# Half products in the output projection of a ViT block: seven instead of eight, with their first operands made in the last chunk of attention

## The chip, the cores and the metric

The kernel runs on one core of a Trainium2 chip. The number that counts is the device time of one execution in microseconds, as the median of three runs. The profile is of one further execution on the same kernel. Engines are called PE (matrix products), DVE (vector), ACT (activations), POOL (GpSimd) and SP (which issues transfers). All tensors are float32.

## The reference

Two layers follow each other on 48 x 48 = 2304 tokens with 768 channels. The first is a transformer block with 12 heads of 64 channels, softmax with relative positions, an output projection and an MLP. The second is a spectral layer (a two-dimensional Fourier transform, a small two-layer network on the modes, and the way back). What the change touches is the step from attention to the MLP:

```python
attn = softmax(q*scale @ k.T + rel_h + rel_w)
out = (attn @ v).transpose(...).reshape(B, H, W, C)
out = out @ proj_w + proj_b          # 2304 x 768 times 768 x 768
x = shortcut + out
xn2 = layernorm(x, ln2_g, ln2_b)
h = gelu(xn2 @ mlp_w1 + mlp_b1)
return x + (h @ mlp_w2 + mlp_b2)
```

## The kernel before, in words

The tokens lie in 18 tiles of 128 (`NT`), the channels in 6 (`NC`), and `CH` = 384 is half of the channels. `main` is one large buffer in SBUF. Through attention it holds exponentials (18 slots of 768 values per partition, `exps`), and then the tokens `x1`, tile n in the place of slot n. `shared` holds `xt` (transposed tokens) and `xs` (three sums of them). `oT` is a buffer in device memory with the output of attention, transposed.

**Attention** runs over 6 pairs of heads (`pr`), in each over 6 chunks of 384 queries (`c`), in each over two runs (`u`) of 9 key tiles: 72 runs. A run makes scores on PE (L525, L531), exponentials on ACT (L535) and one sum on DVE for every key tile but the first (`acc`, L592: 128x768, both inputs in SBUF). The products with the values (L540) of one run are issued in the next. `finish` closes a chunk one run later: `den` on PE (L555), a copy of it with its sum on ACT (L560), then on DVE `ot` (L564), a reciprocal (L567) and the scaled output `o` (L569), then on POOL the running sum `inverse` (L570), and on SP the store into `oT` (L571). The last chunk's `finish` stands after all products. The order of PE and SP inside attention is written by hand (a manual schedule); that of DVE, ACT and POOL is made by a scheduler. Each engine works through its own order without skipping.

**Projection.** For each token tile SP loads a tile of `oT` (`outputs`, `og`, L639, 384 KB) and a tile of x (`residual`, L632), and POOL adds the projection's bias to x (L633). `projected` makes two halves of 384 columns from six products each (L646; two instructions of PE stand behind each product in float32), and DVE adds each half from PSUM to `x1` (L650). Nine tiles (`EARLY`) are projected before a branch. The branch tests that all sums of exponentials and their inverses are below a bound (L666 to L679, on DVE with one transpose on PE), and if they are not, a generic path computes attention again; with this data it is skipped. After the branch the other nine tiles are projected, while tiles 0 to 5 are normalised (L116 to L124), transposed on PE (L132) and written into `xt`; `sums_of_tokens` makes their sums in `xs`. PE's order is written by hand before the branch.

**MLP.** It already forms its products by the scheme of seven half products: `left` makes the sums of one factor's four blocks and `right` those of the other's.

```python
def left(eng, a11, a12, a21, a22, s):
    eng.tensor_tensor(s[0], a21, a22, ALU.add)
    eng.tensor_tensor(s[1], s[0], a11, ALU.subtract)
    eng.tensor_tensor(s[2], a12, s[1], ALU.subtract)
    eng.tensor_tensor(a21, a11, a21, ALU.subtract)

def right(eng, b11, b12, b21, b22, t):
    eng.tensor_tensor(t[0], b12, b11, ALU.subtract)
    eng.tensor_tensor(t[1], b22, t[0], ALU.subtract)
    eng.tensor_tensor(t[2], b21, t[1], ALU.subtract)
    eng.tensor_tensor(b12, b22, b12, ALU.subtract)
```

Of the kernel before, what the change touches and what calls it, by code (L numbers as in the profile page):

```python
# [9 lines left out]
F32 = mybir.dt.float32  # L10
# [3 lines left out]
ALU = mybir.AluOpType  # L14
# [30 lines left out]
def block_then_afno(  # L45
# [139 lines left out]
    with ExitStack() as flag_scope:  # L185
# [9 lines left out]
        pw = col_parts.rearrange("p (c f) -> p c f", c=NC)  # L195

        with ExitStack() as att:
# [108 lines left out]
            def queries_keys_values(qkv):  # L306
# [17 lines left out]
                stage = qkv.enter_context(tc.tile_pool(name="qkv_out", bufs=7))  # L324
# [181 lines left out]
            with tc.manual_schedule(engines={mybir.EngineType.PE, mybir.EngineType.SP}):  # L506
# [44 lines left out]
                def finish(pr, c, acc, ot):  # L551
# [18 lines left out]
                    nc.gpsimd.tensor_tensor(inverse, inverse, rden, ALU.add)  # L570
# [6 lines left out]
                for n, (pr, c, u) in enumerate(runs):  # L577
# [4 lines left out]
                    if (c, u) == (4, 0) and pr == NC - 1:  # L582
                        nc.sync.dma_start(out=pw, in_=proj_w.rearrange("(c p) f -> p c f", p=P))
                    if u == 0:
                        acc = o_pool.tile([P, 2, G], F32, name="acc")
# [44 lines left out]
        def residual(t):  # L630

            nc.sync.dma_start(out=x1[:, t, :], in_=x[ts(t, P), :])  # L632
            nc.gpsimd.tensor_tensor(x1[:, t, :], x1[:, t, :], pb, ALU.add)  # L633

        def outputs(t, og=None):

            if og is None:
                og = pj.tile([P, NC, P], F32, name="og")
            nc.sync.dma_start(out=og, in_=oT[:, ts(t, P)].rearrange("(c p) t -> p c t", p=P))  # L639
            return og  # L640

        def projected(psum, t, og):
            for k in range(2):
                pp = psum.tile([P, CH], F32, name="pp", tag="o")
                for c in range(NC):
                    nc.tensor.matmul(  # L646
                        pp, og[:, c, :], pw[:, c, ts(k, CH)], start=(c == 0), stop=(c == NC - 1)
                    )
                half = x1[:, t, ts(k, CH)]
                nc.vector.tensor_tensor(half, pp, half, ALU.add)  # L650
# [3 lines left out]
        EARLY = NT // 2  # L654
        with tc.tile_pool(name="ps_flag", bufs=1, space=PSUM) as psum, tc.tile_pool(
            name="ps_early", bufs=2, space=PSUM
        ) as psum_early, tc.manual_schedule(engines={mybir.EngineType.PE}):
            early = {t: outputs(t) for t in range(3)}
            pb = pj.tile([P, C], F32, name="pb", bufs=1)
            nc.sync.dma_start(out=pb, in_=proj_b[0, :].partition_broadcast(P))  # L660
            b2 = pj.tile([P, C], F32, name="b2_early", bufs=1)
            nc.sync.dma_start(out=b2, in_=mlp_b2[0, :].partition_broadcast(P))
            residual(0)
            projected(psum_early, 0, early[0])
# [7 lines left out]
            for t in range(1, EARLY):  # L672
# [7 lines left out]
                residual(t)  # L680
                projected(psum_early, t, early[t] if t in early else outputs(t))
            for t in range(EARLY, NT):
                residual(t)
            later = {t: outputs(t) for t in range(EARLY, EARLY + 3)}
# [696 lines left out]
```

## Time and profile before

| | us |
|---|---|
| median of three runs | 3062.45 (3062.34 to 3068.3) |
| the profiled execution, its own time | 3062.51 |
| its span in the profile | 3060.7 |
| QKV, last matmul starts | 450.6 |
| attention, until the last `den` starts | 1522.8 |
| projection, first and last matmul start | 1524.3 and 1677.6 |
| MLP, first and last matmul start | 1678.9 and 2730.1 |
| spectral layer | to the end |

The profile gives for each engine its busy time, and for each group of equal instructions the line, the names of the tiles, the shape and the mean length. A row of a timeline has the start, the length of the group, engine, line, operation, tiles and count, and in brackets the idle time before it with the engine and line that ended the wait. A recorded length runs from the start of an instruction until it is done, and may hold time in which it could not go on. The granted PE clock in that execution was 0.987 of full speed on average.

### The profile page before, as it was taken

How to read it: one execution, taken by the hardware profiler on the slowest of the kernel's cores; microseconds unless marked ns; L12 is line 12 of the kernel's file. 1: busy time of each engine (PE TensorE's matmuls, PEld its weight loads, DVE VectorE, ACT ScalarE, POOL GpSimd, SP SyncE). 2: the span in 40 equal slices, each digit the busy share in tenths (PEclk: the TensorE clock that was granted, in tenths of full speed). 3: DMA queues.
4: the chain of work that ended last, by engine and by line, in shares of the span. 5: the costliest groups of instructions: out<-in, count | busy, mean ns of one | idle time of the engine just before them, and what ended most of it. 6: DMA issues, size and time to landing. Idle time of an engine off the chain costs nothing. (4 is left out here: it accounts for less than half of the span.)

```text
span 3060.7 us, 40413 instructions
## 1 busy us (share of the span) xinstructions
PE 2963.6 (97%) x15495; PEld 1796.0 (59%) x15495; DVE 1783.4 (58%) x2579; ACT 868.6 (28%) x1346; POOL 572.1 (19%) x510
## 2 busy tenths in 40 slices
PE   7999989999999999999999999989999999989998
PEld 4555645655556565555555555545555555548885
DVE  4243217777777777777624766666666566653443
ACT  1011115655556565555400211121101111011110
POOL 2203010000000000000133422342233222311210
PEclk9999999999999999999999999999999999999999
DMA  4433256173452617344332111121112211132324
GB/s 120 132 98 109 96 138 123 28 133 62 81 119 45 136 30 134 66 73 81 110 112 68 52 62 52 53 73 61 53 52 62 74 54 60 52 91 58 87 72 150
DMA packets 204144, 253.37 MB, mean 83 GB/s; under 512 B 21698, under 2 KB 185762, under 8 KB 202406
## 3 DMA queue, kind: packets, MB, share of 16 engines
q1 hardware_dynamic: 203942, 250.69, 32.5%
q8 instruction: 125, 2.05, 0.3%
q14 instruction: 77, 0.63, 0.1%
HBM read 136.77 MB, written 50.14 MB: 61 GB/s over the span
## 5 line engine op out<-in xcount | busy, mean ns | idle before, releaser
L592 DVE TENSOR_TENSOR acc<-acc,main 128x768 f32<-128x768 f32 x576 | 551.8, 958 | 202.6 <-ACT main L535 146.1
L535 ACT ACTIVATE main<-sp 128x768 f32<-128x768 f32 x648 | 522.1, 811 | 155.9 <-PE sp L531 148.6
L531 PE MATMUL sp<-terms,select 64*128 64x384 f32 x1296 | 411.9, 629 | 0.0
L989 DVE TENSOR_TENSOR main<-o,main 128x384 f32<-128x384 f32 x540 | 298.9, 556 | 43.2 <-PE o L987 4.8
L927 PE MATMUL h<-shared,w 128*128 128x384 f32 x864 | 297.1, 487 | 0.8 <-issue 0.8
L417 PE MATMUL m<-main 128*128 128x384 f32 x756 | 253.0, 495 | 23.9 <-DMA main<-in_qkv_w_dram 13.7
L525 PE MATMUL sp<-shared 64*128 64x384 f32 x1296 | 266.4, 488 | 1.6 <-ACT row_hi L223 1.0
L525 PE MATMUL sp<-qT,kT 64*128 64x384 f32 x1296 | 266.4, 487 | 0.0
L570 POOL TENSOR_TENSOR inverse<-inverse,rden 128x384 f32<-128x384 f32 x36 | 46.3, 1286 | 1032.6 <-DVE rden L567 968.9
L927 PEld LDWEIGHTS h<-shared,w 128*128 128x128 f32 x864 | 164.6, 191 | 116.3 <-issue 2.6
L927 PE MATMUL h<-shared,w1s 128*128 128x384 f32 x648 | 226.7, 486 | 0.0
L540 PE MATMUL op<-main,shared 128*64 128x384 f32 x1296 | 221.3, 488 | 0.0
L417 PEld LDWEIGHTS m<-main 128*128 128x128 f32 x756 | 144.4, 193 | 130.1 <-issue 26.1
L540 PE MATMUL op<-main,v 128*64 128x384 f32 x1296 | 220.0, 488 | 0.0
L933 ACT ACTIVATE hT<-c,vec 128x384 f32<-128x384 f32 x108 | 66.4, 615 | 466.5 <-DVE c L939 466.4
L939 DVE TENSOR_TENSOR c<-h,u 128x384 f32<-128x384 f32 x108 | 60.1, 557 | 212.4 <-PE h L927 212.4
L987 PE MATMUL o<-w,hT 128*128 128x384 f32 x432 | 176.3, 490 | 2.9 <-DVE mv L118 1.5
L987 PE MATMUL o<-w2s,hs 128*128 128x384 f32 x432 | 177.2, 492 | 1.0 <-DVE hs L153 1.0
L531 PEld LDWEIGHTS sp<-terms,select 64*128 64x128 f32 x1296 | 125.1, 186 | 83.9
L927 PEld LDWEIGHTS h<-shared,w1s 128*128 128x128 f32 x648 | 123.1, 190 | 85.9
L540 PEld LDWEIGHTS op<-main,v 128*64 128x64 f32 x1296 | 90.6, 138 | 106.4 <-issue 106.4
L525 PEld LDWEIGHTS sp<-shared 64*128 64x128 f32 x1296 | 116.9, 186 | 59.7 <-issue 20.3
(157 smaller groups left out, 3888.7 us busy)
## 6 DMA issues: line engine op xcount, KB each, us to landing
w<-in_mlp_w_dram SPq DMA_DIRECT2D x72, 768.0 KB
terms<-col_parts SPq DMA_DIRECT2D x432, 72.0 KB
terms<-row_hi SPq DMA_DIRECT2D x216, 72.0 KB
terms<-row_lo SPq DMA_DIRECT2D x216, 72.0 KB
main<-in_qkv_w_dram SPq DMA_DIRECT2D x36, 384.0 KB
z<-zt SPq DMA_DIRECT2D x48, 150.0 KB
z<-y SPq DMA_DIRECT2D x50, 144.0 KB
zo<-z SPq DMA_DIRECT2D x12, 600.0 KB
```

The source lines that it names most:

```text
L417: nc.tensor.matmul(bank, a[:, c, :], b[:, c, :], start=(first and c == 0), stop=(c == 2), skip_group_check=not first,)
L525: nc.tensor.matmul(sp[:, j, :G], kT[at, ts(kt, P)], qT[at, ts(c, G)], start=True, stop=False,)
L531: nc.tensor.matmul(sp[:, j, :G], select[at, a % 2], ready[pr, c][at, a // 2, b], start=False, stop=True,)
L535: nc.scalar.activation(p, sp[:, :, :G], AF.Exp, scale=HD**-0.5)
L540: nc.tensor.matmul(op[ts(j, 64)], v[:, kt0 + i, ts(j, 64)], ps[i][:, j, :], start=(kt0 + i == 0), stop=(kt0 + i == NT - 1),)
L570: nc.gpsimd.tensor_tensor(inverse, inverse, rden, ALU.add)
L592: nc.vector.tensor_tensor(acc, made[0] if kt == 1 else acc, p, ALU.add)
L927: nc.tensor.matmul(bank[i], a[:, c, :], b[:, c, :], start=(start and c == 0), stop=(c == 2), skip_group_check=not start,)
L933: nc.scalar.activation(h[:, i, ts(k, G)], src, AF.Gelu, bias=col(V_B1 + 2 * n + i))
L939: nc.vector.tensor_tensor(t, src, other, ALU.add)
L987: nc.tensor.matmul(bank[k], a, b, start=start, stop=True, skip_group_check=not start)
L989: nc.vector.tensor_tensor(dst, bank[k], dst, ALU.add)
```

## The change

The projection works on pairs of token tiles. For a pair, the outputs of attention are a 2 x 2 block matrix (token tile by half of the channels), and so are the weights `pw`; seven products of blocks take the place of eight, each of three matmuls, so 21 matmuls per pair instead of 24. PE makes them in four banks, `o0` to `o3`, of which the fifth, sixth and seventh product use `o0`, `o2` and `o3` a second time. The first product is copied to `u` by ACT, the second is added to `u` by DVE, the third and fourth are added into `x22`, then the second uses of the banks into `x11`, `x21` and `x12`, and at last `u` is added to three of the four quarters.

The sums that the products need are new work. The four sums of the weights (`right`) are made once, on POOL, in the last chunk of attention; they lie in `xs`, and `pw` and the bias `pb` are loaded three runs earlier. The outputs of tiles 0 to 3 are loaded in the last run into `xt`, and the four sums (`left`) of tiles 0 and 1 are made on POOL there. The `left` sums of the other eight pairs are made on DVE. The last chunk's `inverse` is added on DVE.

Ten tiles instead of nine are projected ahead of the branch. `sums_of_tokens` moves to the end of the projection, as `xs` is in use until then. In the first step of the MLP one product with its activation is issued earlier. Pools are reordered or made smaller (five store buffers instead of seven in QKV, fewer in the generic path), and the loads of `b2` and `rows_dft` are issued earlier with that.

The diff, without the parts in the generic path that only make buffers smaller:

```diff
--- before.py
+++ after.py
@@ -193 +193 @@
         pw = col_parts.rearrange("p (c f) -> p c f", c=NC)
+        b11, t3, b21, b22 = (pw[:, ds(3 * i, 3), ts(k, CH)] for i in range(2) for k in range(2))
+        t1, t2, t4 = (xs[:, k] for k in range(3))
+        pb = flag_pool.tile([P, C], F32, name="pb")
+
+        def residual(t):
+
+            nc.sync.dma_start(out=x1[:, t, :], in_=x[ts(t, P), :])
+            nc.gpsimd.tensor_tensor(x1[:, t, :], x1[:, t, :], pb, ALU.add)
+
+        def outputs(t, og):
+
+            nc.sync.dma_start(out=og, in_=oT[:, ts(t, P)].rearrange("(c p) t -> p c t", p=P))
+            return og
+
+        def sums_of_outputs(eng, og, ogs):
+
+            a = [og[i][:, ds(3 * k, 3)] for i in range(2) for k in range(2)]
+            s = [ogs[:, k] for k in range(3)]
+            left(eng, *a, s)
+            return *a, *s
+
+
+        first = [xt.rearrange("p c t -> p (c t)")[:, ts(i, C)] for i in range(4)]
+        first = [a.rearrange("p (c t) -> p c t", c=NC) for a in first]
+        first_parts = []
@@ -324 +349 @@
-                stage = qkv.enter_context(tc.tile_pool(name="qkv_out", bufs=7))
+                stage = qkv.enter_context(tc.tile_pool(name="qkv_out", bufs=5))
@@ -570 +595 @@
                     nc.vector.tensor_tensor(by_rows(o), by_blocks(ot), by_blocks(rden), ALU.mult)
-                    nc.gpsimd.tensor_tensor(inverse, inverse, rden, ALU.add)
+
+                    eng = nc.vector if at == NC * (T // G) - 1 else nc.gpsimd
+                    eng.tensor_tensor(inverse, inverse, rden, ALU.add)
                     nc.sync.dma_start(out=oT[ts(pr, P), ts(c, G)], in_=o)
@@ -583 +610 @@
                     if (c, u) == (4, 0) and pr == NC - 1:
                         nc.sync.dma_start(out=pw, in_=proj_w.rearrange("(c p) f -> p c f", p=P))
+                        nc.sync.dma_start(out=pb, in_=proj_b[0, :].partition_broadcast(P))
+                    if (c, u) == (5, 0) and pr == NC - 1:
+                        right(nc.gpsimd, b11, t3, b21, b22, (t1, t2, t4))
+                    if (c, u) == (5, 1) and pr == NC - 1:
+                        for t in range(4):
+                            outputs(t, first[t])
+                        first_ogs = xt.rearrange("p c t -> p (c t)")[:, ds(4 * C, 9 * P)]
+                        first_ogs = first_ogs.rearrange("p (k c t) -> p k c t", k=3, c=3)
+                        first_parts.append(sums_of_outputs(nc.gpsimd, first[0:2], first_ogs))
                     if u == 0:
                         acc = o_pool.tile([P, 2, G], F32, name="acc")
@@ -628 +664 @@
-        def residual(t):
-
-            nc.sync.dma_start(out=x1[:, t, :], in_=x[ts(t, P), :])
-            nc.gpsimd.tensor_tensor(x1[:, t, :], x1[:, t, :], pb, ALU.add)
-
-        def outputs(t, og=None):
-
-            if og is None:
-                og = pj.tile([P, NC, P], F32, name="og")
-            nc.sync.dma_start(out=og, in_=oT[:, ts(t, P)].rearrange("(c p) t -> p c t", p=P))
-            return og
-
-        def projected(psum, t, og):
-            for k in range(2):
-                pp = psum.tile([P, CH], F32, name="pp", tag="o")
-                for c in range(NC):
+        def loaded(*tiles):
+            return [outputs(t, pj.tile([P, NC, P], F32, name="og")) for t in tiles]
+
+        def ready_parts(og):
+            return sums_of_outputs(nc.vector, og, pj.tile([P, 3, 3, P], F32, name="ogs", bufs=2))
+
+        def projected(psum, t, parts):
+
+            a11, a12, s3, a22, s1, s2, s4 = parts
+            x11, x12, x21, x22 = (x1[:, t + i, ts(k, CH)] for i in range(2) for k in range(2))
+            u = pj.tile([P, CH], F32, name="u", bufs=2)
+            bank = [psum.tile([P, CH], F32, name=f"o{k}", bufs=1) for k in range(4)]
+
+            def product(k, a, b, start, dst=None):
+                for c in range(3):
                     nc.tensor.matmul(
-                        pp, og[:, c, :], pw[:, c, ts(k, CH)], start=(c == 0), stop=(c == NC - 1)
+                        bank[k], a[:, c, :], b[:, c, :], start=(start and c == 0), stop=(c == 2),
+                        skip_group_check=not start,
                     )
-                half = x1[:, t, ts(k, CH)]
-                nc.vector.tensor_tensor(half, pp, half, ALU.add)
-
-
-
-        EARLY = NT // 2
+                if dst is not None:
+                    nc.vector.tensor_tensor(dst, bank[k], dst, ALU.add)
+
+            product(0, a11, b11, True)
+            nc.scalar.copy(u, bank[0])
+            product(1, s2, t2, True, u)
+            product(2, s3, t3, True, x22)
+            product(3, s1, t1, True, x22)
+            product(0, a12, b21, False, x11)
+            product(2, a22, t4, False, x21)
+            product(3, s4, b22, False, x12)
+            for dst in (x12, x21, x22):
+                nc.vector.tensor_tensor(dst, dst, u, ALU.add)
+
+
+
+        EARLY = 10
         with tc.tile_pool(name="ps_flag", bufs=1, space=PSUM) as psum, tc.tile_pool(
             name="ps_early", bufs=2, space=PSUM
         ) as psum_early, tc.manual_schedule(engines={mybir.EngineType.PE}):
-            early = {t: outputs(t) for t in range(3)}
-            pb = pj.tile([P, C], F32, name="pb", bufs=1)
-            nc.sync.dma_start(out=pb, in_=proj_b[0, :].partition_broadcast(P))
             b2 = pj.tile([P, C], F32, name="b2_early", bufs=1)
             nc.sync.dma_start(out=b2, in_=mlp_b2[0, :].partition_broadcast(P))
-            residual(0)
-            projected(psum_early, 0, early[0])
+            for t in range(2):
+                residual(t)
+            projected(psum_early, 0, first_parts[0])
             total = flag_pool.tile([P, 2], F32, name="total")
             nc.vector.tensor_reduce(total[:, 0:1], sums, AX.X, ALU.add)
...
-            for t in range(1, EARLY):
+            for t in range(2, EARLY, 2):
...
-                residual(t)
-                projected(psum_early, t, early[t] if t in early else outputs(t))
+                for i in (t, t + 1):
+                    residual(i)
+                og = first[2:4] if t == 2 else loaded(t, t + 1)
+                projected(psum_early, t, ready_parts(og))
             for t in range(EARLY, NT):
                 residual(t)
-            later = {t: outputs(t) for t in range(EARLY, EARLY + 3)}
+            later = {t: loaded(t, t + 1) for t in (EARLY, EARLY + 2)}
...
@@ -868 +915 @@
-                for t in range(EARLY):
-                    projected(psum, t, outputs(t))
+                for t in range(0, EARLY, 2):
+                    projected(psum, t, ready_parts(loaded(t, t + 1)))
                 for t, og in later.items():
-                    outputs(t, og)
+                    for i in range(2):
+                        outputs(t + i, og[i])
 
         with tc.tile_pool(name="ps_proj", bufs=2, space=PSUM) as psum:
             hats = []
-            for t in range(EARLY, NT):
-                projected(psum, t, later[t] if t in later else outputs(t))
-                n = t - EARLY
-                if n < 6:
+            for t in range(EARLY, NT, 2):
+                projected(psum, t, ready_parts(later[t] if t in later else loaded(t, t + 1)))
+                for n in (t - EARLY, t - EARLY + 1):
+                    if n > 5:
+                        break
                     hats.append(normalise(ln2, x1[:, n, :]))
                     nc.gpsimd.tensor_tensor(x1[:, n, :], x1[:, n, :], b2, ALU.add)
-                if n in (2, 5):
-                    transposed(psum, hats, xt, n // 3, V_LN2G, V_LN2B, tag="t")
-                    hats = []
-                if n == 5:
-                    sums_of_tokens(xt, xs)
+                    if n in (2, 5):
+                        transposed(psum, hats, xt, n // 3, V_LN2G, V_LN2B, tag="t")
+                        hats = []
+            sums_of_tokens(xt, xs)
 
     with ExitStack() as mlp:
+        psum = mlp.enter_context(tc.tile_pool(name="ps_mlp", bufs=1, space=PSUM))
+        hpool = mlp.enter_context(tc.tile_pool(name="mlp_h", bufs=2))
+        upool = mlp.enter_context(tc.tile_pool(name="mlp_u", bufs=2))
+
+        gap = mlp.enter_context(tc.tile_pool(name="gap", bufs=1)).tile([P, 29 * P], F32, name="gap")
+        nc.gpsimd.memset(gap[:, 0:1], 0.0)
+        wpool = mlp.enter_context(tc.tile_pool(name="mlp_w", bufs=2))
         bias = mlp.enter_context(tc.tile_pool(name="mlp_const", bufs=1))
         b2 = bias.tile([P, C], F32, name="b2")
         nc.sync.dma_start(out=b2, in_=mlp_b2[0, :].partition_broadcast(P))
         rows_dft = bias.tile([P, 6, 2 * 2 * KW], F32, name="rows_dft")
         nc.sync.dma_start(out=rows_dft, in_=c_rows)
...
             product(0, a11, b11, True)
             m1 = upool.tile([P, G], F32, name="m1")
             nc.scalar.copy(m1, bank[0])
+            if (p, n) == (0, 0):
+                product(0, a12, b21, False)
+                gelu(0, 0, bank[0])
             product(1, s2, t2, True)
             u = summed(bank[1], m1, "u")
             yield
@@ -952,8 +1005,9 @@
             product(3, s1, t1, True)
             gelu(1, 1, summed(bank[3], u7, "c", 3))
             yield
-            product(0, a12, b21, False)
-            gelu(0, 0, bank[0])
+            if (p, n) != (0, 0):
+                product(0, a12, b21, False)
+                gelu(0, 0, bank[0])
             product(2, a22, t4, False)
             gelu(1, 0, summed(bank[2], u, "c", 3))
             product(3, s4, b22, False)
```

More of the change, by code (lines that the diff above doesn't have):

```diff
@@ L702, in block_then_afno @@
                 q_pool = att.enter_context(tc.tile_pool(name="gen_q", bufs=1))
-                p_pool = att.enter_context(tc.tile_pool(name="gen_p", bufs=2))
+                p_pool = att.enter_context(tc.tile_pool(name="gen_p", bufs=1))
                 s_pool = att.enter_context(tc.tile_pool(name="gen_s", bufs=2))
@@ L756, in block_then_afno @@
                         q_aug = [
-                            q_pool.tile([112, SG], F32, name=f"q_aug{j}", tag=f"q_aug{j}", bufs=2)
+                            q_pool.tile([112, SG], F32, name=f"q_aug{j}", tag=f"q_aug{j}")
                             for j in range(2)
@@ L844, in block_then_afno @@
                                         nc.tensor.transpose(tp[:, i, :], s[:, ts(3 * kg + i, P)], ident)
-                                    pT = s_pool.tile([P, 3, P], F32, name="pT", bufs=4)
+                                    pT = s_pool.tile([P, 3, P], F32, name="pT", bufs=2)
                                     balanced_copy(kg, pT, tp)
@@ L892, in block_then_afno @@
         nc.sync.dma_start(out=rows_dft, in_=c_rows)
-        psum = mlp.enter_context(tc.tile_pool(name="ps_mlp", bufs=1, space=PSUM))
-        hpool = mlp.enter_context(tc.tile_pool(name="mlp_h", bufs=2))
-        upool = mlp.enter_context(tc.tile_pool(name="mlp_u", bufs=2))
-        wpool = mlp.enter_context(tc.tile_pool(name="mlp_w", bufs=2))
         n_f = FF // FCH
```

## The prediction

> **What bounds the kernel now.** I read the page first, then TensorE's (PE's) timeline through the projection, then the vector engine (DVE) and GpSimd (POOL) side by side. The page:
>
> ```profile
> PE 2963.6 (97%) x15495; PEld 1796.0 (59%) x15495; DVE 1783.4 (58%) x2579; ACT 868.6 (28%) x1346; POOL 572.1 (19%) x510
> PE 44%; DVE 2%; DMA 1%; issue 0%; ACT 0%; SPq 0%; DVEq 0%; ACTq 0%
> ```
>
> PE is busy 97% and leads the chain of waits, so fewer matmuls pay at once, unless something makes PE wait. PE's timeline (start, length, line, idle before):
>
> ```profile
> 1511.15 11.78 PE L540 MATMUL op<-main,v 128*64 128x384 f32 x72
> 1522.76 0.81 PE L555 MATMUL den<-acc,ones 128*64 128x384 f32 x4
> 1524.30 8.01 PE L646 MATMUL pp<-col_parts,og 128*128 128x384 f32 x24 [0.73 <-ACT rden L560]
> 1534.25 9.70 PE L646 MATMUL pp<-col_parts,og 128*128 128x384 f32 x24 [1.94 <-DVE main L650]
> 1602.39 25.15 PE L646 MATMUL pp<-col_parts,og 128*128 128x384 f32 x72 [4.14 <-DVEq L686]
> ```
>
> The 18 tiles run unbroken but for two waits, 1.94 us for DVE in tile 1 and 4.14 us at the branch. DVE at that place:
>
> ```profile
> 1504.84 9.46 DVE L592 TENSOR_TENSOR acc<-acc,main 128x768 f32<-128x768 f32 x9 [3.95 <-ACT main L535]
> 1514.22 0.61 DVE L564 SCALAR_TENSOR_TENSOR ot<-rden,vec,ot 128x384 f32<-128x384 f32 x1
> 1517.52 0.56 DVE L569 TENSOR_TENSOR o<-ot,rden 128x384 f32<-128x384 f32 x1
> 1524.28 0.63 DVE L564 SCALAR_TENSOR_TENSOR ot<-rden,vec,ot 128x384 f32<-128x384 f32 x1 [6.21 <-ACT rden L560]
> 1525.02 2.55 DVE L567 RECIPROCAL rden<-rden 128x384 f32<-128x384 f32 x1
> 1534.97 1.72 DVE L671 TENSOR_TENSOR both<-within 128x1 f32<-128x1 f32 x1
> ```
>
> It idles 6.21 us before the last chunk's `ot`; that looks like room. The last row is the warning: 128 values take 1.72 us. POOL then is adding residuals:
>
> ```profile
> 1522.69 9.51 POOL L633 TENSOR_TENSOR main<-main,pb 128x768 f32<-128x768 f32 x5 [3.76 <-DMA main<-in_x_dram]
> 1533.11 22.98 POOL L633 TENSOR_TENSOR main<-main,pb 128x768 f32<-128x768 f32 x13
> ```
>
> The same stretching stands in the QKV stage, where DVE and POOL both add tensors in SBUF:
>
> ```profile
> 300.02 1.36 DVE L159 TENSOR_TENSOR main<-main 128x1152 f32<-128x1152 f32 x1
> 301.29 2.15 DVE L161 TENSOR_TENSOR main<-main 128x1152 f32<-128x1152 f32 x1
> 302.31 1.99 POOL L153 TENSOR_TENSOR main<-main 128x384 f32<-128x384 f32 x1
> ```
>
> The same DVE sum takes 1.36 us alone and 2.15 beside POOL; POOL's 128x384 add, 0.99 alone in other rows, takes 1.99. They take turns, each recorded time holding the wait. DVE's L650 adds, with one input in PSUM, stay at 0.55 us beside the residuals.
>
> **What the Trainium skill says.** "SBUF — State Buffer", section "Who interferes with whom": a DVE instruction with two SBUF inputs contends with a GpSimd instruction that reads SBUF; the shared port pair is held for a whole instruction and the other blocks. The rows above agree. "Perfetto Trace Analysis", section "Tensor Engine Instruction (MATMUL, LD_WEIGHTS)": DVE, ScalarE and GpSimd queues are strict FIFO, so one waiting instruction holds all behind it. The 6.21 us idle agrees: nothing behind `ot` ran. "TensorE: Matmul & The Clock Gate", section "What's actually happening": the clock halves after an idle window of some 3.4 us and returns after a busy one. Here 1.94 us of idle was enough: the 24 matmuls after it took 9.70 us against 24 x 0.3225 = 7.74, so 1.96 us more.
>
> **The change part by part.** Two matmul instructions stand behind each written one; the pitch of an instruction is 3.87/12 = 0.3225 us, 3.87 being the steady spacing of L650.
>
> *Removed.* 3 of 24 matmuls in each of 9 pairs: 27 x 2 x 0.3225 = -17.4 us, all on the path. The wait in tile 1 belonged to the queue of the old flag test and goes with its slow clock: -1.94 - 1.96 = -3.9 (what is late next is the subject below). The branch: DVE's last step is now one SBUF add of 0.55 after the last bank, so +0.5. Unhindered sum: -20.8.
>
> *Added to DVE and ScalarE.* Per pair six PSUM adds, three `u` adds and four left sums, 13 x 0.55 = 7.2 us of a pair's 42 x 0.3225 = 13.5; one ScalarE copy (0.48). These fit once the stage runs.
>
> *Moved to the last chunk.* POOL gets four right sums of 128x1152 (2.61 each by the row of the first weight sums) behind the `inverse` add at 1489.85, and four left sums of 0.99; then residual 0, the next `inverse`, and residuals 1 to 17 (1.80 each). All read SBUF, and DVE in that time makes its seventeen `acc` adds with two SBUF inputs (pitch 1.04). So they take turns. Program order of the changed kernel, followed with a hand-over overlap of 0.1 us (that of the 300 us rows): right sums and the first three adds alternate until 1503, left sums and four more adds until 1510.4, and residual 0 (x lands about 4.15 us after issue, as before) costs 1.8. Two left sums of pair (2,3) also stand ahead of the last add. It ends at 1524.0, not 1514.2. PE's `den` waits for it: the first product starts at 1525.6, so +1.3.
>
> DVE's queue goes on: `ot`, a left sum, reciprocal 2.55, a left sum, then `o` of chunk 4, ending 1529.6 instead of 1518.1. **SP's queue** is in order: the store of this `o` stands there ahead of x 4, x 5 and outputs tile 5. An issue takes 0.38 us (median of x issues), a landing some 4.15 plus what is ahead: tile 5 lands near 1536. (og 0 to 3 and the projection bias are issued early enough, by 1501; pw, 2.3 MB, landed at 1474.) **DVE's next instruction is a left sum of pair (4,5), which waits for tile 5.** Behind it stand two left sums, the last chunk's `ot`, a fourth left sum, reciprocal, `u`, `o`, `inverse` (now on DVE) and only then the first add of bank o2 into x22, which frees o2 for the sixth product. In the meantime x 4 to x 9 land, and POOL has a residual ready for every turn: five DVE instructions each wait up to 1.8. By turns: left sum 1537.1, second 1539.3, third 1541.4, `ot` 1543.7, fourth 1545.8, reciprocal 1548.4, `u` 1548.9, `o` 1549.5, `inverse` 1550.0, reduction 1550.6, x22 1551.1. The sixth product was due at 1525.6 + 5 x 1.935 = 1535.3: PE waits +15.8. The seventh needs the next x22 add, past `within` and `both`, at 1553.0, just in time. Clock after the stop: +2.0.
>
> Sum: -20.8 + 1.3 + 15.8 + 2.0 = -1.7. Later pairs have their sums a pair ahead; residuals 10 to 17 (14.4 us) meet DVE's adds in pair (2,3), whose slack there is two products (3.87 us): 0 to +2, taken as 0.
>
> *Elsewhere.* Five store buffers instead of seven in QKV: a buffer returns after 15.5 us at the nearest, a landing takes about 3, so 0. b2 and rows_dft loaded earlier on SP: 0, queue and memory are free then. MLP's first product pair reordered, token sums moved to the projection's end (they write buffers that now hold the right sums, so follow the last products by at most 2.7 us; the moved product, 1.93, covers most): between -2 and +2 against the 3.3 us that the start of the MLP loses now; I take 0. EARLY 9 to 10 moves work across the branch only.
>
> The profiled execution took 3062.51 us (span 3060.7), level with the median 3062.45, so 3062.5 - 1.7 = 3060.8: **3061 us**.
>
> **Rivals.** *A, the turns cost little.* If the `acc` adds do not block (the trace before never has POOL beside one of L592: 951 to 960 ns always), `o` of chunk 4 ends by 1519.8, tile 5 lands by 1526, the x22 add comes near 1535, a stop of about 1 us: 3062.5 - 20.8 + 1 = **3043**. For it: that gap in the evidence. Against: same operation, same operands as the 2.15 rows. *B, the chain above:* 3056 to 3066. *C, slower.* The same chain, dearer: if hand-overs cost 0.05 instead of saving 0.1, and a landing takes 5 us (x, stores and outputs compete; the DMA ran at 370 to 420 GB/s here), the last `acc` add ends at 1527 and the x22 add at 1558.5: +4.4 for the start, +19.8 for the stop, +2.0, less 20.8, and some 2 in pair (2,3): +7.4, **3070**. The net is about the x22 time minus 1552.8, so it is slower by 0.2% from 1558.9 on. That the sums do not run inside attention at all (the change not doing what it says) is excluded by POOL's program order; the store buffers of QKV as a loss would need landings over 15 us, five times those seen.
>
> **How the numbers follow.** A measurement of this kernel can tell about 0.2%, 6.1 us, from no change. A 0.38, B 0.41, C 0.21. A is all faster; of B, 0.06 lies below 3056.3 and 0.03 above 3068.6; C is slower. So faster 0.44, same 0.32, slower 0.24. B alone spans 3056 to 3066; the range reaches from A's value less 2 for the MLP's start to C's plus 1: 3041 to 3071.
>
> **What would show it.** Right: the last L592 add ends near 1524; POOL rows alternate with DVE's; one PE wait of 12 to 18 us for DVE at 1535 in the sixth product, then matmuls at half clock for about 2 us; seven-product pairs of 13.5 us after it; the left sum of pair (4,5) idle until the DMA of tile 5. Wrong: `acc` adds of 0.96 throughout and a PE stop under 5 us (then A), or an x22 add after 1559 (then C); a new loss at the MLP's start over 4 us would break the zero taken there.

## The result, and the profile after

The change makes the kernel slower by 0.3%: 3069.52 us (3065.36 to 3073.68) against 3059.83 in runs beside it, ratio 1.003 with a 95% interval of 1.0022 to 1.0039, which is 6.7 to 11.9 us. The forecast was 3061, 1.7 less than the 3062.5 from which it started.

The profiled execution took 3067.70 us (span 3065.9). In the profiles here the first matmul of attention starts anywhere between 450.2 and 456.7 us, whichever kernel runs (453.1 before, 451.4 in the changed kernel), so I compare stretches between fixed points rather than spans: the last `den` of attention to the MLP's first product took 161.46 us after and 156.10 before.

The page of the changed kernel, busy time by engine and the chain of waits by engine:

```profile
PE 2951.5 (96%) x15441; PEld 1787.4 (58%) x15441; DVE 1847.8 (60%) x2657; ACT 875.4 (29%) x1357; POOL 592.6 (19%) x518
...
PE 43%; DVE 2%; DMA 1%; issue 0%; ACT 0%; DVEq 0%; ACTq 0%; SPq 0%
```

PE has 54 instructions and 12.1 us of busy time less, DVE 78 and 64.4 us more. 78 adds at 0.55 us would be 43 us: DVE's instructions have become longer too. PE's timeline through the projection (start, length, line, tiles, count, and in brackets the idle time before and what ended it):

```profile
1522.24 0.87 PE L580 MATMUL den<-acc,ones 128*64 128x384 f32 x4 [1.01 <-DVE acc L628]
1527.98 4.21 PE L681 MATMUL o<-col_parts,shared 128*128 128x384 f32 x6 [4.87 <-ACT rden L585]
1531.98 2.85 PE L681 MATMUL o<-shared 128*128 128x384 f32 x6
1534.67 2.10 PE L681 MATMUL o<-col_parts,shared 128*128 128x384 f32 x6
...
1538.54 2.10 PE L681 MATMUL o<-col_parts,shared 128*128 128x384 f32 x6
1548.19 4.21 PE L681 MATMUL o<-shared 128*128 128x384 f32 x6 [7.55 <-DVE main L686]
1552.19 2.98 PE L681 MATMUL o<-col_parts,shared 128*128 128x384 f32 x6
...
1614.09 4.18 PE L681 MATMUL o<-col_parts,og 128*128 128x384 f32 x6 [4.62 <-DVEq L733]
...
1629.05 2.20 PE L681 MATMUL o<-col_parts,ogs 128*128 128x384 f32 x6 [0.78 <-DVE main L686]
...
1645.68 3.81 PE L681 MATMUL o<-shared,og 128*128 128x384 f32 x6 [4.75 <-DVE main L686]
```

A product is six instructions and starts 1.935 us after the last one when nothing is late. So there are four losses: 4.87 us before the first product, for ACT's copy of the last `den`; 7.55 before the sixth, for the first add into `x22`; the branch, 4.62 (4.14 before); and two waits **behind** the branch, 0.78 and 4.75. After each of the longer ones PE runs slowly for up to two products: the first takes 4.00 us from start to start instead of 1.935, and the first two 6.69 (1527.98 to 1534.67) instead of 3.87. I call this a spell of slow clock. DVE in the first part of that time:

```profile
1490.53 2.39 DVE L628 TENSOR_TENSOR acc<-main 128x768 f32<-128x768 f32 x1 [2.09 <-ACT main L560]
1492.84 3.00 DVE L594 TENSOR_TENSOR o<-ot,rden 128x384 f32<-128x384 f32 x1
1495.76 24.41 DVE L628 TENSOR_TENSOR acc<-acc,main 128x768 f32<-128x768 f32 x15
...
1525.88 1.35 DVE L594 TENSOR_TENSOR o<-ot,rden 128x384 f32<-128x384 f32 x1
1535.27 1.10 DVE L152 TENSOR_TENSOR ogs<-og 128x384 f32<-128x384 f32 x1 [8.04 <-DMA og<-oT]
1536.40 2.19 DVE L153 TENSOR_TENSOR ogs<-ogs,og 128x384 f32<-128x384 f32 x1
1538.51 2.16 DVE L155 TENSOR_TENSOR og<-og 128x384 f32<-128x384 f32 x1
...
1547.59 0.55 DVE L686 TENSOR_TENSOR main<-o,main 128x384 f32<-128x384 f32 x1
```

The kernel before at the place of the second and third row:

```profile
1493.09 0.55 DVE L569 TENSOR_TENSOR o<-ot,rden 128x384 f32<-128x384 f32 x1
1493.56 7.33 DVE L592 TENSOR_TENSOR acc<-acc,main 128x768 f32<-128x768 f32 x7
```

The `o` of one chunk takes 3.00 us instead of 0.55; fifteen `acc` adds take 24.41, 1.63 each instead of 1.05. The left sum waits 8.04 us for tile 5, its followers take 2.2 us each, and the add that frees PE's bank ends at 1548.1. GpSimd beside it:

```profile
1492.18 3.24 POOL L159 TENSOR_TENSOR shared<-col_parts,shared 128x1152 f32<-128x1152 f32 x1
...
1526.78 9.17 POOL L203 TENSOR_TENSOR main<-main,pb 128x768 f32<-128x768 f32 x5
```

### The profile page after: what moved, and what is told of

Its sections match the earlier page's. It is cut to its first block, busy times and chain, and to the rows that moved or that the text cites. A ratio compares the mean times of both kernels' runs of the same rounds, so it can differ in the third digit from the quotient of the medians.

```text
span 3065.9 us, 40438 instructions
## 1 busy us (share of the span) xinstructions
PE 2951.5 (96%) x15441; PEld 1787.4 (58%) x15441; DVE 1847.8 (60%) x2657; ACT 875.4 (29%) x1357; POOL 592.6 (19%) x518
## 5 line engine op out<-in xcount | busy, mean ns | idle before, releaser
L628 DVE TENSOR_TENSOR acc<-acc,main 128x768 f32<-128x768 f32 x576 | 560.4, 973 | 197.9 <-ACT main L560 140.8
L442 PE MATMUL m<-main 128*128 128x384 f32 x756 | 252.6, 495 | 23.8 <-DMA main<-in_qkv_w_dram 13.5
L152 POOL TENSOR_TENSOR w1s<-w 128x384 f32<-128x384 f32 x36 | 36.7, 1020 | 613.3 <-DMA w<-in_mlp_w_dram 344.5
```

Source lines behind the costliest of these rows:

```text
L442: nc.tensor.matmul(bank, a[:, c, :], b[:, c, :], start=(first and c == 0), stop=(c == 2), skip_group_check=not first,)
L628: nc.vector.tensor_tensor(acc, made[0] if kt == 1 else acc, p, ALU.add)
```

## The experiments

Stretches are from each kernel's trace. Each ratio is against runs of the kernel before on the same chip; the medians of these, 3059.72 to 3061.38 us, are not shown.

| kernel | median, us | ratio to before (95%) | last `den` to MLP, us | branch to MLP, us |
|---|---|---|---|---|
| before | 3059.83 | | 156.10 | 76.47 |
| changed | 3069.52 | 1.0030 (1.0022, 1.0039) | 161.46 | 69.61 |
| e1_rden2 | 3067.21 | 1.0021 (1.0013, 1.0028) | 160.97 | 69.60 |
| e2_load | 3065.94 | 1.0013 (1.0006, 1.0019) | 159.79 | 69.54 |
| e5_bias | 3056.21 | 0.9987 (0.9979, 0.9995) | 149.09 | 69.47 |
| b2_right | 3063.76 | 1.0011 (1.0000, 1.0022) | 157.09 | 75.09 |
| b1_store5 | 3057.35 | 0.9991 (0.9980, 1.0002) | 154.76 | 77.78 |
| e3_spread | 3065.25 | 1.0015 (1.0007, 1.0023) | 159.27 | 69.45 |
| e6_spread | 3060.33 | 0.9997 (0.9989, 1.0005) | 156.07 | 69.39 |
| e4_parts | 3066.12 | 1.0015 (1.0006, 1.0024) | 157.15 | 67.82 |
| e9_quiet | 3061.04 | 0.9998 (0.9986, 1.0009) | 153.24 | 61.91 |
| e7_both | 3058.30 | 0.9993 (0.9983, 1.0003) | 151.33 | 68.45 |
| e8_hand | 3048.03 | 0.9961 (0.9947, 0.9975) | 142.84 | 68.84 |
| e9_free | 3045.75 | 0.9951 (0.9934, 0.9968) | 138.98 | 65.00 |

(Before, b1_store5 and b2_right have nine tiles left behind the branch, the others eight.)

**What is the 4.87 us wait for?** ACT's copy of the last `den` writes `rden`, which has one buffer. Its row says it waited for L594, the `o` of chunk 4, which still reads the former `rden`:

```profile
1527.35 0.49 ACT L585 ACTIVATE rden<-den 128x384 f32<-128x384 f32 x1 [5.58 <-DVE o L594]
```

```diff
-                    rden = o_pool.tile([P, G], F32, name="rden", bufs=1)
+                    rden = o_pool.tile([P, G], F32, name="rden", bufs=2)
```

> The changed kernel with two buffers for rden instead of one; nothing else. Theory W (three waits in a row, of which the one that ends last decides): the first product no longer waits until 1527.98 for the reader of the former rden and starts 2 to 3 us earlier, but the first add into x22 still ends near 1547.6, as its queue waits for outputs tile 5; the stop before the sixth product grows by what the first wait loses, so the time moves by 0 to -3 us against the changed kernel (less slow clock at most). Rival (each wait costs by itself): -5 to -7 us.

PE's timeline of e1_rden2:

```profile
1525.03 2.20 PE L681 MATMUL o<-col_parts,shared 128*128 128x384 f32 x6 [0.73 <-ACT rden L585]
...
1549.02 4.21 PE L681 MATMUL o<-shared 128*128 128x384 f32 x6 [14.04 <-DVE main L686]
```

The first wait is the single buffer, shown: 0.73 us instead of 4.87. But the sixth product starts only 0.7 us earlier, counted from the start of attention; the time moves into the second wait, 14.04 instead of 7.55. When PE goes on is set by when DVE reaches the `x22` add.

**Is the late tile 5 what makes it late?** Its load is issued first in the block in e2_load.

```diff
+            second = loaded(4, 5)
...
-                og = first[2:4] if t == 2 else loaded(t, t + 1)
+                og = {2: first[2:4], 4: second}[t] if t < 6 else loaded(t, t + 1)
```

> The changed kernel with the loads of outputs tiles 4 and 5 written first in the projection's block, so that SP has them ahead of the store of chunk 4; DVE's order is the same but for three small steps, and POOL's residual 0 now stands behind the inverse of chunk 4. Theory W with turns on the SBUF port: tile 5 is there by 1518, but four left sums, ot, o and inverse still take turns with residuals (about 2.2 us each), x22's first add ends at 1541 to 1544, the stop before the sixth product is 3 to 6 us instead of 7.55, in all -3 to -7 us. Rival (only the late tile 5 counts): that stop is under 1.5 us and the time falls by 9 to 12 us.

DVE's and PE's timelines of e2_load:

```profile
1528.21 2.15 DVE L152 TENSOR_TENSOR ogs<-og 128x384 f32<-128x384 f32 x1
```

```profile
1548.56 4.21 PE L681 MATMUL o<-shared 128*128 128x384 f32 x6 [7.89 <-DVE main L686]
```

Counted from the start of attention, the left sums start 9.6 us earlier, and nothing waits for the load. But the stop is 7.89 us, no shorter (I had expected 3 to 6), and the sixth product comes only 2.1 us earlier. With tile 5 early, all four left sums, `ot` and `inverse` meet a residual add (2.04 to 2.16 us each), and the flag's small steps now stand ahead of the `x22` add. The late tile alone was not the cause.

**Is it the turns with POOL?** e5_bias is e2_load without the residuals' bias adds on POOL.

```diff
-            nc.gpsimd.tensor_tensor(x1[:, t, :], x1[:, t, :], pb, ALU.add)
```

> The kernel of e2_load (outputs tiles 4 and 5 loaded early) with POOL's 18 residual adds left out: the projection's bias is not added to x, so that part of the computation is missing. Theory of turns on the SBUF port: the four left sums, ot, o and inverse behind tile 5 take 0.5 to 0.6 us each instead of 2.15, x22's first add ends 9 to 11 us earlier than in e2_load (near 1538 instead of 1548.5), the stop before the sixth product falls from 7.9 to under 2 us: -8 to -12 us against e2_load. Rival (the length of DVE's queue, not POOL, makes the stop): the stop stays over 5 us, and the time within 3 us of e2_load.

DVE's timeline of e5_bias, and PE's first waits there:

```profile
1529.83 0.55 DVE L152 TENSOR_TENSOR ogs<-og 128x384 f32<-128x384 f32 x1
```

```profile
1530.65 3.90 PE L680 MATMUL o<-col_parts,shared 128*128 128x384 f32 x6 [4.66 <-ACT rden L584]
1604.79 4.18 PE L680 MATMUL o<-col_parts,og 128*128 128x384 f32 x6 [4.34 <-DVEq L733]
```

DVE's order behind tile 5 is that of e2_load. The same sum takes 0.55 instead of 2.15 us, and between the first product and the branch PE has no wait at all. The medians differ by 9.7 us (3061.05 and 3061.07 for the kernel before on the two chips), the stretch to the MLP by 10.7. The turns are the cause of e2_load's stop, shown. In the changed kernel tile 5 is late as well, and a late tile without turns was not run. My estimate from the rows: in e5_bias 2.70 us pass from the first left sum to the reciprocal, and in the changed kernel 4.94 from there to the end of the `x22` add; from 1535.27 on that ends near 1542.9, a stop of some 2.4 us instead of 7.7.

In b2_right the kernel before gets nothing but three right sums of the weights on POOL in the last chunk:

```diff
+                    if (c, u) == (5, 0) and pr == NC - 1:
+                        wb = [pw[:, ds(3 * i, 3), ts(k, CH)] for i in range(2) for k in range(2)]
+                        wt = [xs[:, k] for k in range(3)]
+                        nc.gpsimd.tensor_tensor(wt[0], wb[1], wb[0], ALU.subtract)
+                        nc.gpsimd.tensor_tensor(wt[1], wb[3], wt[0], ALU.subtract)
+                        nc.gpsimd.tensor_tensor(wt[2], wb[2], wt[1], ALU.subtract)
```

> The kernel before with three sums of the projection's weights (128x1152 each, results not used) added on POOL in the last chunk of attention; everything else, the projection in eight half products too, as before. Theory of turns: the sums of acc beside them take 2.5 to 3.5 us each instead of 0.96 recorded, the last chunk's sums end 4 to 8 us later than 1514; as nothing of PE waits for them before 1522.8 and DVE has no left sums behind them, the time rises by only 0 to 3 us. Rival (no port turns): the sums stay at 0.96 us and POOL's at 2.6.

Its DVE timeline:

```profile
1491.50 2.04 DVE L598 TENSOR_TENSOR acc<-main 128x768 f32<-128x768 f32 x1 [2.45 <-ACT main L535]
1493.47 3.00 DVE L569 TENSOR_TENSOR o<-ot,rden 128x384 f32<-128x384 f32 x1
1496.39 19.34 DVE L598 TENSOR_TENSOR acc<-acc,main 128x768 f32<-128x768 f32 x16
```

This settles the point that the kernel before could not show: an `acc` add takes turns like any other, 2.04 us beside a right sum, and `o` 3.00. DVE had caught up before the last `den`, so the start of the projection did not move (1.55 us after `den`, 1.54 before). The ratio of 1.0011 reaches down to 1.0000, so a loss in time is likely and not sure. Its trace also has PE's wait in tile 1 at 3.67 us instead of 1.94: DVE's queue waits there for POOL's last `inverse`, which ends later.

b1_store5 is the kernel before with the five store buffers in QKV (`qkv_out`, 7 to 5).

> The kernel before with five store buffers instead of seven in the QKV stage, nothing else. Prediction's own step (priced 0): within 2 us of the kernel before. Rival (fewer buffers hold up QKV, which would explain part of the loss): QKV ends 2 to 6 us later and the time rises by as much.

It lost nothing: 0.9991, with 1 inside the interval.

**Can the sums lie earlier in attention?** In e3_spread and e6_spread `pw` is loaded at (3, 0), the outputs at (3, 1), and the right sums are spread over the runs from (3, 1) on, with POOL's order fixed by hand. In e3 the fourth right sum and the left sums stand at (5, 0), in e6 at (4, 1).

```diff
-                    if (c, u) == (5, 0) and pr == NC - 1:
-                        right(nc.gpsimd, b11, t3, b21, b22, (t1, t2, t4))
+                        if (c, u) == (3, 1):
...
+                            nc.gpsimd.tensor_tensor(t1, t3, b11, sub)
+                        if (c, u) == (4, 0):
+                            nc.gpsimd.tensor_tensor(t2, b22, t1, sub)
```

> The changed kernel with the same right and left sums on POOL, but one or two at a time from the fourth chunk of the last head pair on (weights loaded one chunk earlier, POOL's order written by hand), not all in the last chunk. Theory of turns: the sums of acc in the last chunk fall back to about 1.05 us each and end near 1515 to 1517 instead of 1522, o of chunk 4 ends 6 to 8 us earlier, the first product starts at 1523 to 1524 without the 4.87 us wait, and x22's first add ends near 1541: -7 to -11 us against the changed kernel. Rival (the longer sums come from something else, for example bandwidth of the loads): sums of acc stay at 1.6 us and the time stays within 2 us.

> As e3_spread, but the fourth right sum and the four left sums of tiles 0 and 1 are also done on POOL before the inverse of chunk 3, so that no POOL sum is left in the last run of attention but residual 0. Theory of turns: the last eight sums of acc take about 1.05 us each (1.9 in e3_spread, 1.6 in the changed kernel), the last ends at 1514 to 1517 instead of 1522, o of chunk 4 ends near 1520, tile 5 lands near 1528, the first product starts at 1523 to 1525, x22's first add ends at 1541 to 1544: -4 to -9 us against the changed kernel. Rival: sums of acc stay above 1.5 us.

e3 missed: at (5, 0) the sums stood behind the `inverse` of chunk 3 in POOL's fixed order, and DVE's scheduler had moved its reciprocal to 1502.8, so they still ran in the last run. e6 got them out of the way. Its DVE and PE timelines:

```profile
1508.97 9.20 DVE L637 TENSOR_TENSOR acc<-acc,main 128x768 f32<-128x768 f32 x8
```

```profile
1527.84 2.20 PE L690 MATMUL o<-col_parts,shared 128*128 128x384 f32 x6 [0.73 <-ACT rden L588]
...
1547.61 4.21 PE L690 MATMUL o<-shared 128*128 128x384 f32 x6 [9.83 <-DVE main L695]
```

The eight adds now take 1.15 us each and the first product waits 0.73 us, even with one `rden` buffer. The stop stays, 9.83 us, since the residuals do. Still, `o` of chunk 4 ends 7.2 us earlier, counted from the start of attention, tile 5 lands 7.7 earlier and the sixth product starts 5.8 earlier: the turns inside attention reach PE by this chain.

**What are the two waits behind the branch?** e4_parts makes the left sums of pairs (10,11) and (12,13) before the branch, with a third `ogs` buffer.

```diff
-            later = {t: loaded(t, t + 1) for t in (EARLY, EARLY + 2)}
+            later = {}
+            for t in (EARLY, EARLY + 2):
+                og = loaded(t, t + 1)
+                later[t] = og, ready_parts(og)
```

> The changed kernel with the left sums of pairs (10,11) and (12,13) made before the branch (a third buffer for them), so that eight fewer of DVE's two-input sums meet POOL's MLP weight sums after it. Theory W: the stops of 4.75 and 0.78 us in pair (12,13) and most of the slow clock behind them go, the branch comes 0 to 2 us later: -4 to -7 us. Rival (normalisation, not the left sums, holds DVE up there): the stop stays over 3 us and the time within 2 us.

One wait of 3.37 us is left of the two, and the stretch falls by 1.8 us. This lies between the theory, by which both waits go, and its rival, by which the time would stay within 2 us: the median falls by 3.4. The scheduler reordered DVE elsewhere too, and of the 4.3 us that the stretch from the last `den` loses, 2.5 lie before the branch. So this alone does not say why the waits are there. e9_quiet asks that: it is the changed kernel without POOL's adds between the branch and the MLP. It leaves out the MLP's bias for six tiles and the sums of the first two weight blocks, whose products read the weights themselves instead.

```diff
-                    nc.gpsimd.tensor_tensor(x1[:, n, :], x1[:, n, :], b2, ALU.add)
...
-            left(nc.gpsimd, a11, a12, a21, a22, [ws[:, i] for i in range(3)])
+            quiet = p == 0 and n < 2
+            if not quiet:
+                left(nc.gpsimd, a11, a12, a21, a22, [ws[:, i] for i in range(3)])
```

> The changed kernel with POOL kept silent between the branch and the MLP: the six adds of the MLP's bias to tiles 0 to 5 (L929) are left out, and the sixteen sums of the first two weight blocks of the MLP (L152 to L161 on POOL) too (the products read the weights themselves in their place). DVE's and PE's order in that stretch stay as they are. Theory T (the waits of 0.78 and 4.75 us behind the branch, and the 1.8 us of slow clock after the second, come from DVE's left sums, u adds and normalisations taking turns with POOL): both waits go, left sums and u adds there take 0.55 each, and the stretch from the branch to the MLP's first product falls from 69.6 to 62 to 63 us; the median falls by 6 to 8 against the changed kernel, to about 3062. Rival L (DVE simply has too many steps in its order ahead of the first bank's add there, with or without POOL): the wait of 4.75 stays above 3, the stretch above 67.

DVE from just before the second wait on, with POOL beside it, in the changed kernel:

```profile
1638.82 1.35 DVE L152 TENSOR_TENSOR ogs<-og 128x384 f32<-128x384 f32 x1
...
1641.36 1.34 DVE L155 TENSOR_TENSOR og<-og 128x384 f32<-128x384 f32 x1
1642.63 1.34 DVE L154 TENSOR_TENSOR ogs<-og,ogs 128x384 f32<-128x384 f32 x1
1643.89 0.54 DVE L686 TENSOR_TENSOR u<-o,u 128x384 f32<-128x384 f32 x1
```

```profile
1638.44 1.31 POOL L154 TENSOR_TENSOR w1s<-w,w1s 128x384 f32<-128x384 f32 x1
...
1642.25 1.30 POOL L161 TENSOR_TENSOR w<-w 128x384 f32<-128x384 f32 x1
```

DVE in e9_quiet, where POOL does nothing in that time:

```profile
1634.76 0.55 DVE L152 TENSOR_TENSOR ogs<-og 128x384 f32<-128x384 f32 x1
...
1636.23 0.55 DVE L155 TENSOR_TENSOR og<-og 128x384 f32<-128x384 f32 x1
1636.70 0.55 DVE L154 TENSOR_TENSOR ogs<-og,ogs 128x384 f32<-128x384 f32 x1
1637.16 0.55 DVE L686 TENSOR_TENSOR u<-o,u 128x384 f32<-128x384 f32 x1
```

The order is the same, the sums are short again, both waits are gone, and the stretch falls from 69.61 to 61.91 us, where the theory of turns said 62 to 63. The windows view of the same 43 us (busy PE, PEld, DVE, ACT, POOL; then PE's clock and DMA), first the changed kernel, then e9_quiet, whose first product behind the branch starts 2.6 us later:

```profile
1612.00:1655.00 43.00, 35.38 (x104) 20.51 (x105) 35.63 (x63) 5.41 (x12) 26.93 (x20) 0.88 0.33 111
```

```profile
1612.00:1655.00 43.00, 38.50 (x124) 23.10 (x124) 30.93 (x71) 6.47 (x13) 0.00 (x0) 0.92 0.33 111
```

DVE does 71 instructions in 30.93 us instead of 63 in 35.63.

**Versions meant to be faster.** e7_both joins e6_spread, the second `rden` buffer, and e4's early left sums, made on POOL for the first two pairs behind the branch.

> e6_spread, with two buffers for rden, and with the left sums of pairs (10,11) and (12,13) made on POOL before the branch, after the residuals; DVE's order then has o and inverse of the last chunk ahead of the left sums of pair (4,5). Theory W (three waits, each ended by the shared port): first product near 1523, stop before the sixth product under 4 us, no stop over 2 us behind the branch, slow clock behind them gone: -14 to -20 us against the changed kernel, that is 3049 to 3055 and faster than the kernel before. Rival (seven products cost as much elsewhere as they save): not faster than the kernel before.

The stop before the sixth product is 5.54 us and one of 3.16 is left behind the branch; I had expected under 4 and a time of 3049 to 3055. The left sums of pair (2,3) waited on DVE until 1526 for memory that PE's products of attention still read, and so met the residuals again.

e8_hand also fixes the order of DVE and POOL in the first five pairs. The principle is a queue: each PSUM add, which frees a bank, goes first, and one SBUF add is put behind it.

```diff
                 if dst is not None:
                     nc.vector.tensor_tensor(dst, bank[k], dst, ALU.add)
+                    if dst is x21 or dst is x12 or (dst is x22 and k == 3):
+                        queue.append(partial(nc.vector.tensor_tensor, dst, dst, u, ALU.add))
+                    for _ in range(0 if not hand or t == 0 and dst is u else 2 if last else 1):
+                        pop()
```

The left sums of the next pair stand in the same queue, those behind the branch are made on POOL, residuals 0 and 1 lie in the last run, the last `inverse` is on POOL again, the flag is formed later, and `u` has three buffers. These were changed together, so the share of each is not shown.

> e7_both with DVE's and POOL's order in the first five pairs written by hand: left sums and u adds stand one at a time behind the adds that free a bank, residuals 0 and 1 are made in the last run of attention, the last inverse is on POOL again, the flag is formed two pairs later; and the left sums of the last two pairs are on POOL, too. Theory W: no stop before the sixth product (under 1 us), the first product about 1.5 us behind den, at most one stop under 2 us behind the branch; from den to the MLP's first product 141 to 146 us against 156.1 before and 161.5 in the changed kernel, so 10 to 15 us faster than the kernel before (3046 to 3052). Rival (two-input adds and residuals fill the port, whatever the order): stops of 4 us or more come back in pair (2,3), and the time is within 3 us of e7_both.

Its PE timeline:

```profile
1527.21 2.20 PE L710 MATMUL o<-col_parts,shared 128*128 128x384 f32 x6 [0.74 <-ACT rden L606]
...
1599.65 3.78 PE L710 MATMUL o<-col_parts,og 128*128 128x384 f32 x6 [4.34 <-DVEq L775]
...
1668.49 4.18 PE L1020 MATMUL h<-shared,w 128*128 128x384 f32 x6 [7.71 <-DMA w<-in_mlp_w_dram]
```

PE runs through 35 products up to the branch without a wait, although the residual adds still make DVE's SBUF adds 1.2 to 1.7 us long: while they do, at most one of these stands between two adds that PE needs, and a product takes 1.935. A new wait of 7.71 us comes at the MLP's start, for a weight load that SP can't issue until the last `u` add has left the memory that it takes. e9_free puts `u` into a pool of its own, ahead of the others:

```diff
+        pu = flag_scope.enter_context(tc.tile_pool(name="proj_u", bufs=3))
         pj = flag_scope.enter_context(tc.tile_pool(name="proj", bufs=6))
...
-            u = pj.tile([P, CH], F32, name="u", bufs=3)
+            u = pu.tile([P, CH], F32, name="u")
```

> The hand-ordered version (e8_hand) with one further edit: the buffers u lie in a pool of their own ahead of the others of the projection, so that the memory at the end of it, which the first weight tile of the MLP takes, was last used by an earlier pair. If the 7.71 us wait at the MLP's first product came from that tile's load waiting for the last u add, the load is issued tens of us earlier, the wait falls below 2 us, and the median falls by 7 to 11 us against e8_hand, to 3037 to 3042 (ratio to the kernel before 0.993 to 0.994). If the load then waits for another late buffer, the wait stays and so does the 3048. If the weight sums, now earlier on POOL, take turns with DVE behind the branch, part comes back there: waits of 1 to 4 us in the last three pairs.

The load is issued 2.2 us after the start of the last product instead of 5.0, still late (in the changed kernel some 66 us ahead of it): SP issues it when PE's last product ends, which reads another buffer of that pool. The wait at the MLP's start is 4.96 us. From the last `den` to the MLP the gain is 3.9 us, not the 7 to 11 expected; by the medians it is 2.3, but the intervals of the two ratios overlap. At 3045.75 it has the lowest median here, 15.6 us below before in its own comparison.

## Why the prediction was wrong

**The unhindered part held.** The 27 matmuls fewer, the old wait and its slow clock were priced at -21.3 us. In e9_free, which has a full run of products up to the branch, the last `den` to the MLP is 17.1 us below before with a 5.0 us wait still in it. One reading was a little off: the 9.70 us of the 24 slow matmuls run to the end of the last one, so they stand against the row of 8.01, or 9.54 to the start of what follows against 7.74. The slow clock there cost 1.8 us, not 1.96.

**Start and stop: the sum held, its parts did not.** The prediction had +1.3 for the start of the first product, +15.8 for the stop, +2.0 for the clock, 19.1 in all. Measured: the last `den` starts 1.2 later in attention's own time, and the first product another 4.2 after it, 5.4; the slow clock behind that 2.8; the stop 7.7 (1548.19 against 1540.48 due); its slow clock 3.0: 18.9. The mechanism was right. To set the trace against the forecast, which is in the time of the kernel before, 1.7 us are added to it, as attention began that much earlier: the last `acc` add ended at 1523.8 (forecast 1524.0), `o` of chunk 4 at 1528.9 (1529.6), tile 5 landed at 1537.0 (1536), left sums of up to 2.2 us followed, and the `x22` add ended at 1549.8 (1551.1). One step failed without changing the sum, "PE's `den` waits for it: the first product starts at 1525.6": it followed `den` to its last reader but not the buffer that ACT copies it into. With one `rden`, ACT had to wait for the `o` of chunk 4, and the product started at 1529.7. That this hardly changes the total was shown by e1_rden2: PE then waits at the sixth product instead. By the text's own rule, net equals the `x22` time less 1552.8, the kernel should have come out 3.0 us faster, and 2.0 with the slow clock of 3.0 in place of 2.0: near the forecast -1.7. So up to the branch the forecast held, and only the near cancelling of these two misses of about 1 us was luck.

**The step that failed, and decided the sign, is "These fit once the stage runs".** It summed DVE's added adds at 0.55 us, 7.2 of a pair's 13.5, and took the later pairs at 0. It carried the turns only through the residuals, up to pair (2,3). Behind the branch POOL adds the MLP's bias to six tiles and makes the sums of its first two weight blocks; before, DVE had no two-input SBUF adds in that time to meet them. Now it has the left sums and `u` adds, and the normalisations stretch too. The waits cost 1.0 and 4.9 against the pitch, and 1.8 of slow clock follows: 7.7 us where 0 was forecast, and 7.7 is what e9_quiet took away. The view that shows it beforehand is POOL's own timeline behind the branch, 28 us of adds between 1607 and 1637 in the kernel before, of which these are the first and the last:

```profile
1607.77 1.00 POOL L152 TENSOR_TENSOR w1s<-w 128x384 f32<-128x384 f32 x1 [51.67 <-DMA og<-oT]
1608.72 1.80 POOL L880 TENSOR_TENSOR main<-main,b_early 128x768 f32<-128x768 f32 x1
...
1632.52 3.95 POOL L880 TENSOR_TENSOR main<-main,b_early 128x768 f32<-128x768 f32 x2 [1.05 <-DVE hat L124]
```

**The smaller terms.** The branch, with the slow clock behind it, and the first product of the MLP cost 1.3 together (0.5 and 0 forecast), the MLP stage up to the spectral layer's first product 0.9 (0). The store buffers cost nothing, as said. The sum of all is -21.3 + 18.9 + 7.7 + 1.3 + 0.9 = +7.5 us from the start of attention to the end of the MLP, against the -1.7 forecast; the medians' interval of +6.7 to +11.9 holds it. The spans differ by less, 5.2, since in the profiled execution attention began 1.7 us earlier and what follows the MLP took 0.6 less.

**The rivals.** A, that turns cost little, is refuted by e5_bias and b2_right. B's chain took place. C came nearest in time (3070) but not by its mechanism: it had the chain dearer before the sixth product, and the loss lay behind the branch.

The Trainium skill's statement in "SBUF — State Buffer", section "Who interferes with whom", that the shared port pair is held for a whole instruction, agrees with the left sums of 2.04 to 2.16 us beside residual adds of 1.80; the mistake was to apply it to one stage only.

## What to carry to other kernels

When a change gives DVE adds with both inputs in SBUF, list every stretch in which GpSimd reads SBUF, to the end of the stage, and price each meeting with a whole GpSimd instruction, not with DVE's own time. Then put first in DVE's order what frees a bank for PE, and only behind it what may be stretched: with all of them in front of a bank's add the stop was 5.5 to 14 us here, with one behind each there was none. And for each late step, ask not only who reads its result but which single buffer it must fill.

## What the runs showed of the hardware

The turns are strict: in e2_load every left sum beside residual adds of 1.80 us took 2.04 to 2.16, its own 0.55 plus one whole add less about 0.2. One DVE step with a single large SBUF input stretches as well: the normalising TENSOR_SCALAR of 128x768 takes 0.67 us in e9_quiet and 0.82 to 1.35 beside POOL's adds in the changed kernel. The statistics ahead of it (BATCH_NORM_STATS2, 128x384) do not: 0.50 to 0.56 in both.

The slow clock behind a wait costs a spell, not a share. Counted from start to start over two products, or over the 24 matmuls of tile 1, it is 1.8 us after a wait of 1.94 in the kernel before, 3.0 after 3.16 in e7_both, 1.8 after 4.75, 2.8 after 4.87 and 3.0 after 7.55 in the changed kernel, and 3.0 after 14.04 in e1_rden2. In b1_store5 a wait of 1.35 us in tile 1 cost none (24 matmuls in 8.01). From these numbers I estimate that two waits of 4 us are dearer than one of 8.
